# Four chained image layers on one core: the layer norms' inverse deviations are spread by DMA, and the last image's pointwise products use 64x64 array tiles

## The chip, the cores and the metric

The kernel runs on one core of a Trainium2 chip. The metric is the time of one execution in microseconds, measured on the device. Before the change it is 2722.68 us, the median of three runs from 2719.42 to 2723.97.

The core's engines are named as in the profile: PE (TensorE, matrix products; PEld is its loading of weights, which overlaps), DVE (VectorE), ACT (ScalarE), POOL (GpSimd) and SP (SyncE, here only an issuer of DMAs). Each engine runs its own list of instructions in order, and waits where an operand isn't ready. SBUF is the on-chip memory of 128 partitions; PSUM holds the results of PE.

## The reference, cut to what matters

Four images of 64x64 positions with 64 channels go through four layers. Layers 0, 2 and 3 are attention over the 4096 positions of an image (in layer 2 a position's row and column play the parts of space and channel as the reference reshapes them). Layer 1, which is changed here, is a convolution block with two layer norms:

```python
def _ln(x, g, b):
    m = jnp.mean(x, axis=-1, keepdims=True)
    v = jnp.mean(jnp.square(x - m), axis=-1, keepdims=True)
    return (x - m) * jax.lax.rsqrt(v + EPS) * g + b

y = _ln(x, ln1_g, ln1_b)
y = _pw(y, pw1_w, pw1_b)              # 64 -> 256 channels at each position
y = _dw3x3(y, dw_w, dw_b)
y1, y2 = jnp.split(y, 2, axis=-1)
y = y1 * y2
w = jnp.mean(y, axis=(1, 2), keepdims=True)
w = _pw(w, sca_w, sca_b)
y = y * w
y = _pw(y, pw2_w, pw2_b)
x = x + y * beta
z = _ln(x, ln2_g, ln2_b)
z = _pw(z, pw3_w, pw3_b)              # 64 -> 256 channels
z1, z2 = jnp.split(z, 2, axis=-1)
z = z1 * z2
z = _pw(z, pw4_w, pw4_b)
return x + z * gamma
```

All data is float32.

## The kernel before

An image is kept as X[:, b], 128 partitions by 2048 columns: partitions 0 to 63 are the 64 channels of one half of the positions, partitions 64 to 127 those of the other half. A group of 512 columns is called j (0 to 3), a half s (0 or 1), and tok(x, s, j) takes one such block of 64 partitions by 512 columns.

The kernel has two paths: fast_path, which is what runs here, and a general path that is taken only if a check of value ranges at the end fails. Everything below is fast_path.

The order of work on PE, ACT and DVE is written out by a program-level scheduler. A main list, items, holds the attention work: a layer 0 item is the scores of 128 positions (L1008, then exponentials L1012 on ACT), a layer 2 item the scores L1207 with exponentials L1215, a layer 3 item L1321 with L1326. Work that is due some items later (products L1032, L1224, L1348; evictions of accumulators, L1039 on DVE; the scaling vq, L1021 to L1024 on DVE) is put behind the item it is due at. Beside the list two lanes, conv and misc, are generators whose yield says how many units of about a microsecond to let pass before their next piece. After an item's scores and again after its due work, each lane ticks by the item's own number of units and issues the pieces whose time has come. conv runs layer1(b) for the four images one after another, starting when image b's layer 0 is through its items; it runs beside layer 0 of the next image, and for the last images beside layer 2. misc runs the preparation of the attention layers: project0, features2 (which copies ko between halves by DMA on SP, L1190), close2 and open3 (which copies keys ph from tg by DMA on SP, L1295).

PE works on parts of its array. A product with 64 rows of weights uses one row half, so that two of them (s = 0 and 1) run beside each other: "64*128" in the profile's lines. Layer 2's scores and products use quarters, "64*64", four beside each other. In layer 0 the scores are 64*128 and the products 128*64.

PSUM has three buffers of 128x1024 for scores and everything else (new_ps) and two of 128x512 for attention's accumulators (new_acc). In SBUF, tiles t and u share two buffers (new_t), and xn has one.

The norm (called twice in layer1) works so: ACT squares X (L1058); PE sums X and its squares over the channels with the matrix jsel, 1/64 in column s for the partitions of half s (L1064), which leaves means and mean squares at rows 32j+s of a PSUM tile; ACT, DVE and ACT turn these into the inverse deviation (L1069 to L1072), at rows 32j+s of t. To multiply a channel, the inverse deviation of its positions has to be on that channel's partition. PE does this with the matrix bsel, the transpose of the selection sel: for each j it multiplies 32 rows of bsel with 32 rows of t (L1078), which gives a 128x512 block, two blocks per PSUM tile. DVE then multiplies the PSUM tile with X into xn (L1083). The mean itself isn't subtracted there; it is folded into the weights pw1 and pw3 in setup (cmat, L903).

The pointwise products that follow are L1103 (pw1, written to the padded tile by ACT at L1108, then convolved by DVE at L1123 and L1125) and L1160 (pw3, joined by ACT L1165 and DVE L1167 into u; then pw4, L1171). Each uses, for one j and one half r of the outputs, two matmuls of 64 weight rows by 128 outputs, one for each s.

In the profile a float32 matmul appears as two instructions.

Of the kernel before, what the change touches and what calls it, by code (L numbers as in the profile page):

```python
# [8 lines left out]
F32 = mybir.dt.float32  # L9
# [682 lines left out]
def fast_path(ctx: ExitStack, tc: tile.TileContext, a: dict, out: bass.AP, bad):  # L692
    nc = tc.nc
    B, H, W, C = a["x"].shape
# [4 lines left out]
    const = ctx.enter_context(tc.tile_pool(name="const", bufs=1))  # L699
# [11 lines left out]
    def new_ps(name="ps"):  # L711
        return pp.tile([128, 1024], F32, tag="ps", name=name)
# [7 lines left out]
    def new_t(name="t"):  # L720
        return tp.tile([128, 1024], F32, tag="t", name=name)
# [7 lines left out]
    mm = nc.tensor.matmul  # L729
# [8 lines left out]
    def fetch_x(b, queues):  # L738
# [19 lines left out]
        out=gam0, in_=a["L0_conv_gamma"].rearrange("(o n) -> o n", o=1).to_broadcast([128, 1])  # L758
# [3 lines left out]
    ident = const.tile([128, 128], F32, name="ident")  # L762
# [40 lines left out]
    for nm in names128:  # L803
        r = flat[nm].shape[0] // 128
        nc.sync.dma_start(
            out=rows[col[nm] : col[nm] + r, :], in_=flat[nm].rearrange("(r c) -> r c", r=r)
        )
    for nm in names64 + names32:
        n = flat[nm].shape[0]
        nc.sync.dma_start(  # L810
            out=rows[col[nm] : col[nm] + 1, :].rearrange("o (d n) -> o d n", n=n),
            in_=flat[nm].rearrange("(r d n) -> r d n", r=1, d=1).to_broadcast([1, 128 // n, n]),
# [11 lines left out]
    pw1 = blocks("pw1", "L1_conv_pw1_w", 256, [(0, 0), (1, 0)], 256)  # L824
# [16 lines left out]
    bqk = const.tile([128, 1], F32, name="bqk")  # L841
    cmat = const.tile([128, 128], F32, name="cmat")
    nc.gpsimd.memset(cmat, 0.0)
    sel = new_t("sel")[:, 0:128]
    nc.gpsimd.memset(sel, 0.0)
    for s in range(2):
        nc.gpsimd.memset(cmat[64 * s : 64 * s + 64, 64 * s : 64 * s + 64], -1.0 / C)
        nc.gpsimd.memset(sel[64 * s : 64 * s + 64, s:128:32], 1.0)
    jsel = const.tile([128, 32], F32, name="jsel")
    bsel = const.tile([128, 128], F32, name="bsel")  # L850
    eps1 = const.tile([128, 1], F32, name="eps1")
    nc.gpsimd.memset(eps1, EPS1)
    eps3 = const.tile([128, 1], F32, name="eps3")
# [22 lines left out]

    def setup():
        nc.vector.tensor_add(cmat, cmat, ident)
        nc.vector.tensor_scalar_mul(jsel, sel[:, 0:32], 1.0 / C)
        ps = new_ps()  # L880
        nc.tensor.transpose(ps[:, 0:128], sel, ident)
        nc.tensor.transpose(ps[:, 512 : 512 + n_rows], rows, ident[:n_rows, :n_rows])
        nc.vector.tensor_copy(bsel, ps[:, 0:128])
        nc.vector.tensor_copy(vec, ps[:, 512 : 512 + n_rows])
        yield 5.0

        ps = new_ps()
        for i, (w_, sh, bi) in enumerate(
            ((pw1, "L1_conv_ln1_b", "L1_conv_pw1_b"), (pw3, "L1_conv_ln2_b", "L1_conv_pw3_b"))
        ):  # L890
            for r in range(2):
                mm(
                    ps[:, 2 * i + r : 2 * i + r + 1], w_[0:64, bass.ts(r, 128)], V(sh, 0, 0, 64),
                    start=True, stop=True,
                )
            nc.vector.tensor_add(
                pwb[:, i, :], ps[:, 2 * i : 2 * i + 2], vec[:, col[bi] : col[bi] + 2]
            )

        ps = new_ps()  # L900
        for i, (w_, g) in enumerate(((pw1, "L1_conv_ln1_g"), (pw3, "L1_conv_ln2_g"))):
            nc.vector.tensor_scalar_mul(w_, w_, V(g))
            mm(ps[:, 512 * i : 512 * i + 256], cmat, w_, start=True, stop=True)  # L903
            nc.vector.tensor_copy(w_, ps[:, 512 * i : 512 * i + 256])
        nc.vector.tensor_mul(resb[:, 0:1], V("L1_conv_pw2_b"), V("L1_conv_beta"))
        nc.vector.tensor_mul(resb[:, 1:2], V("L1_conv_pw4_b"), V("L1_conv_gamma"))
        yield 3.0
# [15 lines left out]
    def tok(x, s, j):  # L923
        return x[64 * s : 64 * s + 64, bass.ts(j, 512)]
# [128 lines left out]
    def norm(x, y):  # L1053


        sq = [new_t("sq"), new_t("sq")]
        for i in range(2):
            act(sq[i], x[:, bass.ts(i, 1024)], AF.Square)  # L1058
        yield 4.0
        ps = new_ps()  # L1060
        for i, src in enumerate(((x, x), (sq[0], sq[1]))):
            for j in range(4):
                c = 512 * j if i == 0 else 512 * (j % 2)
                mm(  # L1064
                    ps[32 * j : 32 * j + 32, bass.ts(i, 512)], jsel, src[j // 2][:, c : c + 512],
                    start=True, stop=True,
                )
        t = new_t()
        act(t[:, 0:512], ps[:, 0:512], AF.Square)  # L1069
        stt(t[:, 0:512], t[:, 0:512], -1.0, ps[:, 512:1024], ALU.mult, ALU.add)  # L1070
        act(t[:, 0:512], t[:, 0:512], AF.Ln, bias=eps1)
        act(t[:, 512:1024], t[:, 0:512], AF.Exp, scale=-0.5)  # L1072
        yield 7.0
        for jp in range(2):
            ps = new_ps()
            for i in range(2):
                p = 32 * (2 * jp + i)
                mm(  # L1078
                    ps[:, bass.ts(i, 512)], bsel[p : p + 32, :], t[p : p + 32, 512:1024],
                    start=True, stop=True,  # L1080
                )
            cols = bass.ts(jp, 1024)
            nc.vector.tensor_mul(y[:, cols], ps, x[:, cols])  # L1083
            yield 3.5

    def layer1(b):
        x = X[:, b]
        y = xn.tile([128, 2048], F32, tag="xn", name="xn")
        yield from norm(x, y)
        yg = new_big("yg")[:, 0:N].rearrange("p (w h) -> p w h", h=H)  # L1090
        ysum = sm.tile([128, 4], F32, tag="ysum", name="ysum")
        for r in (1, 0):
            pad = new_pad()
            nc.gpsimd.memset(pad[:, 0:PW], 0.0)
            nc.gpsimd.memset(pad[:, 65 * PW : 66 * PW + 2], 0.0)
            nc.gpsimd.memset(
                pad[:, PW : 65 * PW].rearrange("p (w h) -> p w h", h=PW)[:, :, 0:1], 0.0
            )
            inner = pad[:, PW + 1 : 65 * PW + 1].rearrange("c (p q s h) -> c q p s h", p=2, s=2, h=PW)
            for j in range(4):  # L1100
                ps = new_ps()
                for s in range(2):
                    mm(  # L1103
                        ps[:, bass.ts(s, 512)], pw1[64 * s : 64 * s + 64, bass.ts(r, 128)],
                        tok(y, s, j), start=True, stop=True,
                    )
                for s in range(2):
                    act(  # L1108
                        inner[:, bass.ts(j, 4), :, s, 0:H],
                        ps[:, bass.ts(s, 512)].rearrange("c (q p h) -> c q p h", p=2, h=H),  # L1110
                        AF.Identity, bias=pwb[:, 0, r : r + 1],
                    )
                yield 3.5
            for j in range(4):
                w0 = 16 * j
                y2 = yg[:, w0 : w0 + 16, :]
                out_ = y2 if r else new_t("y1").rearrange("p (w h) -> p w h", h=H)
                for k in range(9):
                    o = (w0 + k % 3) * PW + k // 3
                    win = pad[:, o : o + 16 * PW].rearrange("p (w h) -> p w h", h=PW)[:, :, 0:H]  # L1120
                    wt = V("L1_conv_dw_w", 2 * k + r)
                    if k == 0:
                        nc.vector.tensor_scalar(out_, win, wt, V("L1_conv_dw_b", r), ALU.mult, ALU.add)  # L1123
                    else:
                        stt(out_, win, wt, out_, ALU.mult, ALU.add)  # L1125
                    yield 1.8
                if not r:
                    stt(y2, out_, 1.0, y2, ALU.mult, ALU.mult, accum_out=ysum[:, j : j + 1])
                    yield 1.8
# [3 lines left out]
        ps = new_ps()  # L1133
# [6 lines left out]
        for j in range(4):  # L1140
            ps = new_ps()
# [13 lines left out]
        for j in range(4):  # L1155
            t, u = new_t(), new_t("u")
            for r in range(2):
                ps = new_ps()
                for s in range(2):
                    mm(  # L1160
                        ps[:, bass.ts(s, 512)], pw3[64 * s : 64 * s + 64, bass.ts(r, 128)],
                        tok(z, s, j), start=True, stop=True,
                    )
                if r == 0:
                    act(t, ps, AF.Identity, bias=pwb[:, 1, 0:1])  # L1165
                else:
                    stt(u, ps, pwb[:, 1, 1:2], t, ALU.add, ALU.mult)  # L1167
                yield 3.5
            ps = new_ps()
            for s in range(2):  # L1170
                mm(ps[64 * s : 64 * s + 64, 0:512], pw4, u[:, bass.ts(s, 512)], start=True, stop=True)  # L1171
            act(t[:, 0:512], ps[:, 0:512], AF.Identity, bias=resb[:, 1:2], scale=V("L1_conv_gamma"))
            xs = x[:, bass.ts(j, 512)]
            nc.vector.tensor_add(xs, xs, t[:, 0:512])
            yield 3.5
# [424 lines left out]
```

## Time and profile before

| what | value |
|---|---|
| median of three runs | 2722.68 us |
| the profiled execution: its own time, its span | 2720.37 us, 2718.6 us |
| granted clock of PE, mean | 0.994 |
| norm sums L1064 on PE, X and squares | 8.5 and 8.3 us busy, 64 instructions each |
| spreading L1078 on PE | 18.0 us busy, 64 instructions |
| product L1083 on DVE | 19.5 us busy, 16 instructions of 1222 ns |
| pointwise L1103, L1160 on PE | 35.8 and 35.0 us busy, 128 instructions each |
| DMA over the whole span | 24.33 MB; queue of SP 3.1% of 16 engines' span |

The span goes from the first to the last instruction of the execution. Busy times of PE count every instant at which a matmul is under way, so that matmuls side by side count once; single durations (about 600 ns for 512 columns) overlap and can't be summed. A timeline line gives start, duration, engine, line, and how many instructions were merged; in brackets stands how long the engine was idle before, and what ended it. A windows line gives, for each engine, busy time and number of instructions in a stretch, then the granted clock of PE, the share of the DMA engines, and GB/s.

### The profile page before, as it was taken

Reading aid. Unit: us, or ns where it says so; the run is one execution under the profiler, and the core shown is the slowest. Engines: PE = TensorE matmul, PEld = TensorE weight load, DVE = VectorE, ACT = ScalarE, POOL = GpSimd, SP = SyncE. Lnnn points to the kernel's source line nnn. Section 1 sums busy time; section 2 is a strip of 40 time slices with the busy share of each in tenths; the row PEclk is TensorE's granted clock in tenths of the full one; section 3 lists DMA queues with packets and bytes.
Section 4 is the critical chain, followed back from the end, with each engine's and each line's share of the span. In section 5 each row is a group of like instructions: output and inputs, shape, how many; then the busy total and the mean of one; then the engine's idle time right before and its main releaser. Section 6 shows DMA issues by size and latency. Waiting matters only on the chain.

```text
span 2718.6 us, 41825 instructions
## 1 busy us (share of the span) xinstructions
PE 2656.8 (98%) x18042; PEld 902.6 (33%) x18042; DVE 1349.0 (50%) x1507; ACT 1724.6 (63%) x2796; POOL 16.6 (1%) x66
## 2 busy tenths in 40 slices
PE   8999999999999999999999999999999999999996
PEld 3343333333333333323333332243322333322222
DVE  3232478437773478216720027920058700088888
ACT  4545655565556555555655668855678756578886
POOL 2000000000000000000000000000000000000000
PEclk9999999999999999999999999999999999999998
DMA  3000000000000000000010000010000010010001
GB/s 71 0 1 1 1 1 1 1 1 1 1 1 1 8 8 1 1 1 17 1 32 1 16 1 1 1 32 1 17 1 1 1 32 1 1 32 1 1 1 64
DMA packets 17349, 24.33 MB, mean 9 GB/s; under 512 B 2460, under 2 KB 10885, under 8 KB 17157
## 3 DMA queue, kind: packets, MB, share of 16 engines
q1 hardware_dynamic: 16085, 20.47, 3.1%
q8 instruction: 143, 2.34, 0.4%
q0 software_dynamic: 672, 0.56, 0.1%
q10 hardware_dynamic: 400, 0.56, 0.1%
q14 instruction: 49, 0.40, 0.0%
HBM read 4.80 MB, written 4.19 MB: 3 GB/s over the span
## 4 chain that ended last, share of the span: by engine, by line
PE 94%; DVE 4%; ACT 2%; issue 0%; DMA 0%; ACTq 0%; DVEq 0%
PE acc L1032 17%; PE ps L1008 17%; PE acc L1224 16%; PE ps L1207 16%; PE ps L1321 11%; PE acc L1348 9%; PE ps L1103 1%; PE ps L1160 1%; PE accz L1337 1%; PE ps L1078 1%; PE ps L1143 1%; PE ps L1171 1%; PE ps L1064 1%; PE ps L1302 1%; PE ps L985 1%; DVE tg L1344 0%
## 5 line engine op out<-in xcount | busy, mean ns | idle before, releaser
L1012 ACT ACTIVATE e<-ps 128x1024 f32<-128x1024 f32 x512 | 517.1, 1024 | 343.4 <-PE ps L1008 231.0
L1215 ACT ACTIVATE e<-ps 128x1024 f32<-128x1024 f32 x512 | 517.1, 1024 | 308.1 <-PE ps L1207 308.0
L1326 ACT ACTIVATE e<-ps 128x1024 f32<-128x1024 f32 x512 | 495.4, 1022 | 94.9 <-PE ps L1321 85.1
L1344 DVE TENSOR_TENSOR tg<-tg,e 128x2048 f32<-128x2048 f32 x214 | 490.4, 2292 | 26.1 <-ACT e L1326 7.4
L1008 PE MATMUL ps<-X,q 64*128 64x512 f32 x2048 | 482.7, 608 | 11.3 <-ACT e L1012 4.2
L1207 PE MATMUL ps<-ko 64*64 64x512 f32 x4096 | 470.4, 593 | 7.8 <-ACT ko L1189 5.5
L1224 PE MATMUL acc<-e,X 64*64 64x512 f32 x4096 | 468.0, 591 | 2.7 <-DVE X L1039 2.1
L1032 PE MATMUL acc<-e,vq 128*64 128x512 f32 x2048 | 468.4, 599 | 0.0
L1321 PE MATMUL ps<-tg,ph 32*128 32x512 f32 x2048 | 321.2, 640 | 0.5 <-ACT e L1326 0.5
L1039 DVE SCALAR_TENSOR_TENSOR yv<-acc,gam,yv 128x512 f32<-128x512 f32 x224 | 168.0, 750 | 290.4 <-PE acc L1032 278.6
L1008 PEld LDWEIGHTS ps<-X,q 64*128 64x128 f32 x2048 | 187.0, 187 | 295.3 <-issue 190.1
L1348 PE MATMUL acc<-e,tg 128*32 128x512 f32 x2048 | 272.0, 603 | 1.3 <-ACT yz L1354 1.3
L1207 PEld LDWEIGHTS ps<-ko 64*64 64x64 f32 x4096 | 156.4, 133 | 294.7 <-issue 196.4
L1224 PEld LDWEIGHTS acc<-e,X 64*64 64x64 f32 x4096 | 159.6, 133 | 280.3 <-issue 265.0
L1032 PEld LDWEIGHTS acc<-e,vq 128*64 128x64 f32 x2048 | 136.6, 137 | 311.7 <-issue 290.3
L1232 DVE TENSOR_TENSOR ph<-ph,acc 128x512 f32<-128x512 f32 x16 | 11.0, 688 | 423.7 <-ACT ph L1231 423.7
L1321 PEld LDWEIGHTS ps<-tg,ph 32*128 32x128 f32 x2048 | 103.2, 182 | 219.2 <-issue 139.9
L1125 DVE SCALAR_TENSOR_TENSOR yg<-pad,vec,yg 128x1024 f32<-128x1024 f32 x128 | 164.3, 1283 | 5.9 <-ACT pad L1108 2.4
L1125 DVE SCALAR_TENSOR_TENSOR y<-pad,vec,y 128x1024 f32<-128x1024 f32 x128 | 164.3, 1284 | 3.7
L1348 PEld LDWEIGHTS acc<-e,tg 128*32 128x32 f32 x2048 | 43.5, 108 | 190.6 <-issue 185.1
L1215 ACT ACTIVATION_READ_ACCUMULATOR e<-ps 128x1 f32 x512 | 106.0, 207 | 0.0
L1012 ACT ACTIVATION_READ_ACCUMULATOR e<-ps 128x1 f32 x512 | 106.0, 207 | 0.0
(187 smaller groups left out, 996.5 us busy)
## 6 DMA issues: line engine op xcount, KB each, us to landing
ph<-tg SPq DMA_DIRECT2D x64, 128.0 KB
ko<-ko SPq DMA_DIRECT2D x16, 256.0 KB
out_dram<-o SPq DMA_DIRECT2D x8, 512.0 KB
xr<-in_x_dram SPq DMA_DIRECT2D x14, 256.0 KB
xr<-in_x_dram ACTq DMA_DIRECT2D x2, 256.0 KB
pw<-in_L_conv_pw_w_dram POOLq DMA_DIRECT2D x4, 64.0 KB, 4.6
sca<-in_L_conv_sca_w_dram POOLq DMA_DIRECT2D x1, 64.0 KB, 6.2
pw<-in_L_conv_pw_w_dram POOLq DMA_DIRECT2D x2, 32.0 KB, 4.8
```

The lines of the kernel that those rows point to most:

```text
L1008: mm(ps[:, bass.ts(r, 512)], m.q[rows_, bass.ts(t, 128)], x[rows_, bass.ts(g, 512)], start=True, stop=True,)
L1012: act(es[g // 2][:, bass.ts(g % 2, 1024)], ps, AF.Exp, bias=SHIFT0, accum_out=zs[:, g : g + 1],)
L1032: mm(accs[g][64 * r : 64 * r + 64, :], vq, es[half][:, 1024 * g + 512 * r : 1024 * g + 512 * r + 512], start=t == 2 * p, stop=t == 2 * p + 1,)
L1039: stt((x if p == 15 else m.y)[:, cols], accs[g], gam0, (m.y if p else x)[:, cols], ALU.mult, ALU.add,)
L1125: stt(out_, win, wt, out_, ALU.mult, ALU.add)
L1207: mm(ps[64 * c : 64 * c + 64, bass.ts(r, 512)], m.ko[rows_, 128 * jb + 64 * c : 128 * jb + 64 * c + 64], m.ko[rows_, bass.ts(2 * ib + r, 5 ...
L1215: act(es[n, jb], ps, AF.Exp, bias=SHIFT2, accum_out=m.zs[:, jb, ib : ib + 1])
L1224: mm(acc[r][64 * c : 64 * c + 64, :], xw[rows_, jb, :], es[n, jb][rows_, bass.ts(c, 512)], start=jb == 0, stop=jb == 31,)
L1321: mm(tiles[k // 2][:, bass.ts(k % 2, 512)], m.ph[rows_, bass.ts(mc, 128)], m.th[rows_, bass.ts(nb, 512)], start=True, stop=True,)
L1326: act(e[:, bass.ts(kp, 1024)], tiles[kp], AF.Exp)
L1344: nc.vector.tensor_add(esum, esum, e)
L1348: mm(st["y"][32 * k : 32 * k + 32, :], m.gx[:, mc, :], e[:, bass.ts(k, 512)], start=mc == 0, stop=mc == 31,)
```

## The change

There are two edits. In norm, the two pairs of L1078 products and their PSUM tiles are gone. SP issues eight DMAs instead, one for each j and half h: each takes one row of t (512 values on partition 32j+h) and writes it to the 64 partitions of that half in y, the tile xn. After a yield of 14 units DVE multiplies y in place with X, in two pieces of 1024 columns, with yields of 1.8 instead of 3.5. bsel is no longer needed: jsel is written directly on POOL, and setup loses a transpose and two small DVE operations.

In layer1, both pointwise layers go through a new function, pointwise. For images 0 to 2 it issues the same two matmuls as before; for the last image it splits the 128 outputs in two, which gives four matmuls of 64 rows by 64 outputs.

```diff
@@ setup of constants
-    sel = new_t("sel")[:, 0:128]
-    nc.gpsimd.memset(sel, 0.0)
+    jsel = const.tile([128, 32], F32, name="jsel")
+    nc.gpsimd.memset(jsel, 0.0)
     for s in range(2):
         nc.gpsimd.memset(cmat[64 * s : 64 * s + 64, 64 * s : 64 * s + 64], -1.0 / C)
-        nc.gpsimd.memset(sel[64 * s : 64 * s + 64, s:128:32], 1.0)
-    jsel = const.tile([128, 32], F32, name="jsel")
-    bsel = const.tile([128, 128], F32, name="bsel")
+        nc.gpsimd.memset(jsel[64 * s : 64 * s + 64, s : s + 1], 1.0 / C)
@@ def setup():
         nc.vector.tensor_add(cmat, cmat, ident)
-        nc.vector.tensor_scalar_mul(jsel, sel[:, 0:32], 1.0 / C)
         ps = new_ps()
-        nc.tensor.transpose(ps[:, 0:128], sel, ident)
         nc.tensor.transpose(ps[:, 512 : 512 + n_rows], rows, ident[:n_rows, :n_rows])
-        nc.vector.tensor_copy(bsel, ps[:, 0:128])
         nc.vector.tensor_copy(vec, ps[:, 512 : 512 + n_rows])
@@ def norm(x, y):
         act(t[:, 512:1024], t[:, 0:512], AF.Exp, scale=-0.5)
         yield 7.0
+        for j in range(4):
+            for h in range(2):
+                nc.sync.dma_start(
+                    out=y[64 * h : 64 * h + 64, bass.ts(j, 512)],
+                    in_=t[32 * j + h : 32 * j + h + 1, 512:1024].unsqueeze(1).to_broadcast([1, 64, 512]),
+                )
+        yield 14.0
         for jp in range(2):
-            ps = new_ps()
-            for i in range(2):
-                p = 32 * (2 * jp + i)
-                mm(
-                    ps[:, bass.ts(i, 512)], bsel[p : p + 32, :], t[p : p + 32, 512:1024],
-                    start=True, stop=True,
-                )
             cols = bass.ts(jp, 1024)
-            nc.vector.tensor_mul(y[:, cols], ps, x[:, cols])
-            yield 3.5
+            nc.vector.tensor_mul(y[:, cols], y[:, cols], x[:, cols])
+            yield 1.8
@@ def layer1(b):
         x = X[:, b]
+        width = 64 if b == B - 1 else 128
+
+        def pointwise(ps, w, r, src, j):
+            for o in range(0, 128, width):
+                for s in range(2):
+                    mm(
+                        ps[o : o + width, bass.ts(s, 512)],
+                        w[64 * s : 64 * s + 64, 128 * r + o : 128 * r + o + width],
+                        tok(src, s, j), start=True, stop=True,
+                    )
+
...
                 ps = new_ps()
-                for s in range(2):
-                    mm(
-                        ps[:, bass.ts(s, 512)], pw1[64 * s : 64 * s + 64, bass.ts(r, 128)],
-                        tok(y, s, j), start=True, stop=True,
-                    )
+                pointwise(ps, pw1, r, y, j)
...
                 ps = new_ps()
-                for s in range(2):
-                    mm(
-                        ps[:, bass.ts(s, 512)], pw3[64 * s : 64 * s + 64, bass.ts(r, 128)],
-                        tok(z, s, j), start=True, stop=True,
-                    )
+                pointwise(ps, pw3, r, z, j)
```

## The prediction

> **What bounds the kernel now.** I read the page first: engine shares, then the chain that ended last.
>
> ```profile
> span 2718.6 us, 41825 instructions
> PE 2656.8 (98%) x18042; PEld 902.6 (33%) x18042; DVE 1349.0 (50%) x1507; ACT 1724.6 (63%) x2796; POOL 16.6 (1%) x66
> PE 94%; DVE 4%; ACT 2%; issue 0%; DMA 0%; ACTq 0%; DVEq 0%
> ```
>
> TensorE (PE) is the bound: 98% busy, 94% of the chain, only 61.8 us idle in the span. So a matmul taken away is worth its slot on PE, and any wait on which PE stands is paid in full. VectorE is half idle over the span, but PE's accumulators are emptied by it. Next, the timeline around the first norm (image 0), which has every piece that the change touches:
>
> ```profile
> 288.47 1.06 PE L1064 MATMUL ps<-X,jsel 128*32 128x512 f32 x8
> 289.35 1.04 PE L1064 MATMUL ps<-sq,jsel 128*32 128x512 f32 x8
> 290.32 2.85 PE L1008 MATMUL ps<-X,q 64*128 64x512 f32 x12
> ...
> 292.69 0.63 ACT L1072 ACTIVATE t<-t 128x512 f32<-128x512 f32 x1
> ...
> 299.01 1.13 PE L1078 MATMUL ps<-t,bsel 32*128 32x512 f32 x4
> 300.07 3.70 PE L1008 MATMUL ps<-X,q 64*128 64x512 f32 x16
> ...
> 303.70 1.13 PE L1078 MATMUL ps<-t,bsel 32*128 32x512 f32 x4
> 304.76 1.13 PE L1103 MATMUL ps<-xn,pw 64*128 64x512 f32 x4
> ```
>
> Call T0 the end of the norm's sums on PE (290.3). The inverse deviation is ready at T0+3.0 (292.69+0.63). A pair of L1078 products holds PE for 1.06 us, start to next start (299.01 to 300.07, 303.70 to 304.76). One "step" of attention work, scores or products, is 3.6 us.
>
> Then the only copies between SBUF partitions of the size that the change adds: ph<-tg, 16 of 128 KB each. SyncE's timeline and the windows (last two columns: share of the 16 DMA engines, GB/s):
>
> ```profile
> 1396.97 11.32 SPq L1295 DMA_DIRECT2D ph<-tg  x16
> ...
> 1398.00:1400.00 2.00, 2.00 (x18) 0.66 (x12) 0.00 (x0) 0.00 (x0) 0.00 (x0) 1.00 0.80 170
> 1404.00:1406.00 2.00, 2.00 (x21) 1.10 (x22) 1.24 (x2) 0.19 (x1) 0.00 (x0) 1.00 0.95 208
> ```
>
> They go out every 0.71 us (11.32/16), data flows some 1.2 us after the first issue, at 208 GB/s at best with the engines 95% busy. Last, what a PE pause costs beyond itself, where layer 2's layout is first built (last columns: granted clock, DMA share, GB/s):
>
> ```profile
> 954.15 3.78 PE L1008 MATMUL ps<-X,q 64*128 64x512 f32 x8 [3.14 <-ACT ko L1189]
> 957.87 4.76 PE L1032 MATMUL acc<-e,vq 128*64 128x512 f32 x16
> ...
> 954.00:958.00 4.00, 3.85 (x10) 1.27 (x12) 1.54 (x2) 3.35 (x8) 0.00 (x0) 0.50 0.61 131
> 958.00:962.00 4.00, 4.00 (x14) 1.19 (x16) 0.17 (x1) 1.10 (x2) 0.00 (x0) 0.73 0.00 0
> ```
>
> After 3.1 us of idleness the clock is half: 8 matmuls take 3.78 us instead of half of 3.70, the next 16 4.76 instead of 3.65. That is 1.9+1.1 = about 3 us extra per pause.
>
> [...]ph<-tg uses 32 partitions[...], and 208 is its best window. No single-partition copy is in the trace. [...]four 64x64 quads take 3.48 us between like neighbours (1128.52 to 1132.00, 0.87 each), a lone 64x128 pair among them 1.06 (1412.85 to 1413.91).[...]
>
> **The change, part by part.**
> (1) Removed: 8 norms x 2 pairs of L1078 = 16 slots x 1.06 = -17.0 us on PE (the group's busy time is 18.0). All of it is on the path.
> (2) Setup: one transpose (0.33 us) and two small VectorE operations go: -0.5 with its start; the memsets on GpSimd are off the path.
> (3) Last image: 16 pairs become 64x64 quads. In both kernels all of image 3's pointwise work falls beside layer 2, which runs in 64x64: 16 x (1.06-0.87) = -3.0. Bounds: [...]-5 if the neighbours' steps shorten also (3.60 to 3.48).
> Sum of gains: 20.5 us.
> (4) VectorE's product reads SBUF instead of PSUM: L1083 takes 1222 ns, and an all-SBUF product of that size (L1514) 1220. Nothing.
> (5) Pacing: each norm's lane gets 14+3.6 instead of 7 units after it, two norms per image: about +21 units per image, +85 by image 3. Layer 1 ended at 1445 and so ends near 1530, before layer 3's first scores at 1609, beside which VectorE and ScalarE would be over 80% busy (108 and 110 us of the first 131). Nothing in time.
> (6) Added: 8 copies per norm of 128 KB, each one row of one partition sent to 64. SyncE issues them one behind the other, the first waiting for the exponential. The ko and ph copies of layers 2 and 3 are behind them on that queue; they are consumed tens of us later, and cost nothing.
> (7) The new wait: VectorE's two products wait for copies 1-4 and 5-8. Behind the second on VectorE are the accumulator evictions (L1039) and the scaling of vq; behind these, PE.
>
> What the copies cost is the whole question. From below: at ph<-tg's rate the last issues at T0+3.0+7x0.71 and lands 1.9 later, at T0+10. The instruction order of the changed kernel puts VectorE's products some five to seven steps after T0, 18 us or later: hidden, cost zero. From above: copies 1-4 read partitions 0, 1, 32, 33[...]; 5-8 read 64, 65, 96, 97[...]. [...]landed at T0+4.2+19.0+0.3 = T0+23.5 and T0+42.5; products done at 24.7 and 43.7. I take this end[...].
>
> PE's stalls follow from its new order (steps of 3.6, a pointwise pair 1.0, 1.2 us of ScalarE delay as at 294):
> - Norm 1: first pair wanted at 22.8, free at 24.7; a step and pair later attention products need the accumulators whose eviction is behind the second product: wanted 30.3, free 43.7+1.5 (evictions)+0.6 (vq) = 45.8. Stall 1.9+15.5 = 17.4.
> - Norms 2 and 3: seven steps before the first pair (26.4), accumulators wanted at 32.0: 13.8 each.
> - Norm 4: stops at pw4's product, wanted 35.6, its input after evictions, vq and L1167: 47.0. 11.4.
> - Norm 5: third pair wanted 35.6, ready 43.7, then 1.1 for accumulators: 9.2.
> - Norms 6 to 8, beside layer 2: only five steps before the first pair, 19.1 against 24.7: 5.6; then pw4's product or the third pair: 11.1, 10.0, 11.1. Together 16.7, 15.6, 16.7.
> Sum 114.6. Eleven of these pauses exceed 3 us: 11 x 2.9 = 32 for the clock. Total cost 147.
>
> Net: -20.5+147 = +126. The profiled execution took 2720.4 (span 2718.6): 2847 us. The median before, 2722.7, is 2 us above it, less than the scatter of its three runs.
>
> **The rivals.**
> Hidden copies: the single rows are read about as fast as ph<-tg. For it: [...]the same 2 KB is read again and again. [...]Then only the gains remain: 2720.4-20.5 = 2700, the side opposite to my forecast. It decides where the second half lands before about T0+28 (products 1.2, evictions 1.5, against 32): 1.05 MB in 24 us, some 44 GB/s.
> Partly hidden: a rate between 30 and 44, for instance if the engines run unevenly and the two halves overlap. The stall of each norm shrinks towards the 2.6 us (20.5/8) that only cancels the gains: 2700 to 2800.
> Slower than a port: [...]Each half takes 19 us more, so the last product comes 38 later: +304, about 3150. Nothing in the trace excludes it; nothing shows it.
> The copies do carry the same values as bsel did (row 32j+h to half h), so the change does what it says.
>
> **How the numbers follow.** One port 0.55 (2847, own range 2800 to 2890: clock 1 to 4 us a pause, halves overlapping a little); hidden 0.22; partly hidden 0.10; slower than a port 0.13. The range 2696 to 2890 takes in the first three and leaves out the last (0.13) and the tails (some 0.05). Faster by over 0.2% (5.4 us, what a measurement of this kernel can tell from none): 0.22. Within: 0.03, from the partly hidden case. Slower: 0.55+0.13+0.07 = 0.75.
>
> **What will show it.** In the changed profile: VectorE waiting for xn's copies, some 100 us or more in 16 waits; DMA at 25 to 30 GB/s for about 38 us from each norm's exponential; PE idle before the attention products and pointwise pairs, followed by the half clock; no L1078 matmuls. A lone quad in image 3 should hold PE about 0.87. I am wrong if the copies' windows show over 45 GB/s: then PE never waits and the time falls by about 20.

## The result, and the profile after

| | before | after |
|---|---|---|
| median | 2722.66 us (4 runs) | 2815.40 us (4 runs) |
| span of the profiled execution | 2718.6 us | 2814.0 us |
| PE busy, idle in the span | 2656.8, 61.8 us | 2660.4, 153.6 us |
| mean granted clock of PE | 0.994 | 0.975 |

The changed kernel is slower: ratio 1.0343, interval 1.0325 to 1.0361, 92.7 us. The direction and the cause were as forecast, the size was 31 to 34 us less than forecast. The page of the changed kernel, with the lines that answer to those of before:

```profile
span 2814.0 us, 41965 instructions
PE 2660.4 (95%) x18041; PEld 915.8 (33%) x18041; DVE 1347.6 (48%) x1505; ACT 1725.1 (61%) x2796; POOL 16.5 (1%) x66
PE 85%; DVE 4%; SPq 4%; DMA 3%; ACT 2%; issue 2%; ACTq 0%; DVEq 0%; POOL 0%; POOLq 0%
L1078 DVE TENSOR_TENSOR xn<-xn,X 128x1024 f32<-128x1024 f32 x16 | 19.6, 1225 | 212.9 <-DMA xn<-t 212.9
```

PE's share of the chain has fallen from 94% to 85%; SP's queue, which was not listed before, and the DMA, which was at 0%, now hold 7% of it. In front of its 16 products VectorE stands idle for 212.9 us in all and waits for the copies. (Lines have moved: L1078 is now this product, L1071 the copies, L1088 both pointwise layers, L1034 the evictions, L1165 the product u, L1003 and L1027 layer 0's scores and products.)

The first norm's copies, in SP's timeline and in the windows (last columns: granted clock, DMA share, GB/s):

```profile
293.40 26.93 SPq L1071 DMA_DIRECT2D xn<-t  x8
```

```profile
300.00:304.00 4.00, 4.00 (x20) 1.45 (x18) 0.42 (x3) 3.75 (x7) 0.00 (x0) 1.00 0.95 28
...
312.00:316.00 4.00, 1.73 (x10) 0.46 (x7) 1.47 (x2) 0.00 (x0) 0.00 (x0) 0.96 0.89 43
316.00:320.00 4.00, 4.00 (x12) 1.87 (x14) 1.55 (x5) 1.92 (x3) 0.00 (x0) 0.61 0.94 28
```

The 16 DMA engines are 95% busy and move 28 GB/s. Only where the first half of the copies ends and the second, from other rows, begins does a window show more, 43 GB/s. The eight copies take SP 26.93 us to issue, a median of 4.36 us each over all 64, where ph<-tg took 0.71: SP's issuing was slow where the copies were slow. VectorE and PE in the same norm:

```profile
314.53 1.23 DVE L1078 TENSOR_TENSOR xn<-xn,X 128x1024 f32<-128x1024 f32 x1 [6.82 <-DMA xn<-t]
315.67 1.41 DVE L1034 SCALAR_TENSOR_TENSOR yv<-acc,gam,yv 128x512 f32<-128x512 f32 x2
...
332.22 1.23 DVE L1078 TENSOR_TENSOR xn<-xn,X 128x1024 f32<-128x1024 f32 x1 [14.60 <-DMA xn<-t]
```

```profile
315.86 2.08 PE L1088 MATMUL ps<-xn,pw 64*128 64x512 f32 x4 [2.27 <-issue]
317.69 4.31 PE L1003 MATMUL ps<-X,q 64*128 64x512 f32 x16
...
322.79 3.65 PE L1027 MATMUL acc<-e,vq 128*64 128x512 f32 x16
333.55 2.08 PE L1088 MATMUL ps<-xn,pw 64*128 64x512 f32 x4 [7.10 <-issue]
335.39 5.69 PE L1003 MATMUL ps<-X,q 64*128 64x512 f32 x16
```

T0, the end of the sums on PE, is 290.4 here. The two halves are there at T0+24.1 and T0+41.8. PE stands 2.3 and 7.1 us before the first and the third pointwise pair; after each pause the scores take 4.31 and 5.69 us in place of 3.70, at a granted clock of 0.61 (316 to 320) and 0.50 (332 to 336): the half clock. In the next norm PE stands before attention's products instead, which need VectorE's evictions queued behind its second product:

```profile
584.77 5.61 PE L1027 MATMUL acc<-e,vq 128*64 128x512 f32 x16 [12.82 <-DVE yv L1034]
```

### The profile page after: what moved, and what is told of

It is laid out like the page before. It is cut to its first block, busy times and chain, and to the rows that moved or that the text cites. A ratio compares the mean times of both kernels' runs of the same rounds, so it can differ in the third digit from the quotient of the medians.

```text
span 2814.0 us, 41965 instructions
## 1 busy us (share of the span) xinstructions
PE 2660.4 (95%) x18041; PEld 915.8 (33%) x18041; DVE 1347.6 (48%) x1505; ACT 1725.1 (61%) x2796; POOL 16.5 (1%) x66
## 2 busy tenths in 40 slices
DMA packets 22471, 32.74 MB, mean 12 GB/s; under 512 B 3484, under 2 KB 11909, under 8 KB 22277
## 4 chain that ended last, share of the span: by engine, by line
PE 85%; DVE 4%; SPq 4%; DMA 3%; ACT 2%; issue 2%; ACTq 0%; DVEq 0%; POOL 0%; POOLq 0%
PE acc L1027 15%; PE acc L1222 15%; PE ps L1003 14%; PE ps L1205 14%; PE ps L1319 10%; PE acc L1346 8%; SPq L1071 4%; DMA xn<-t 3%; PE ps L1088 2%; PE accz L1335 1%; ACT e L1213 1%; DVE y L1127 1%; PE ps L1169 1%; PE ps L1145 1%; PE ps L1059 1%
## 5 line engine op out<-in xcount | busy, mean ns | idle before, releaser
L1213 ACT ACTIVATE e<-ps 128x1024 f32<-128x1024 f32 x512 | 516.7, 1024 | 309.6 <-PE ps L1205 309.5
L1003 PE MATMUL ps<-X,q 64*128 64x512 f32 x2048 | 483.7, 609 | 22.7 <-DVE u L1165 12.1
L1027 PE MATMUL acc<-e,vq 128*64 128x512 f32 x2048 | 473.0, 604 | 25.3 <-DVE yv L1034 25.3
L1034 DVE SCALAR_TENSOR_TENSOR yv<-acc,gam,yv 128x512 f32<-128x512 f32 x224 | 167.5, 750 | 290.0 <-PE acc L1027 278.6
L1003 PEld LDWEIGHTS ps<-X,q 64*128 64x128 f32 x2048 | 189.2, 188 | 307.1 <-issue 198.7
L1222 PEld LDWEIGHTS acc<-e,X 64*64 64x64 f32 x4096 | 166.9, 134 | 274.6 <-issue 256.0
L1027 PEld LDWEIGHTS acc<-e,vq 128*64 128x64 f32 x2048 | 137.7, 138 | 340.6 <-issue 290.2
L1078 DVE TENSOR_TENSOR xn<-xn,X 128x1024 f32<-128x1024 f32 x16 | 19.6, 1225 | 212.9 <-DMA xn<-t 212.9
L1088 PE MATMUL ps<-xn,pw 64*128 64x512 f32 (+1 forms) x320 | 77.3, 690 | 45.2 <-issue 45.0
L1213 ACT ACTIVATION_READ_ACCUMULATOR e<-ps 128x1 f32 x512 | 106.1, 207 | 0.0
```

Source lines behind the costliest of these rows:

```text
L1003: mm(ps[:, bass.ts(r, 512)], m.q[rows_, bass.ts(t, 128)], x[rows_, bass.ts(g, 512)], start=True, stop=True,)
L1027: mm(accs[g][64 * r : 64 * r + 64, :], vq, es[half][:, 1024 * g + 512 * r : 1024 * g + 512 * r + 512], start=t == 2 * p, stop=t == 2 * p + 1,)
L1034: stt((x if p == 15 else m.y)[:, cols], accs[g], gam0, (m.y if p else x)[:, cols], ALU.mult, ALU.add,)
L1213: act(es[n, jb], ps, AF.Exp, bias=SHIFT2, accum_out=m.zs[:, jb, ib : ib + 1])
L1222: mm(acc[r][64 * c : 64 * c + 64, :], xw[rows_, jb, :], es[n, jb][rows_, bass.ts(c, 512)], start=jb == 0, stop=jb == 31,)
```

## The experiments

Each experiment was compared with the kernel before on the same chip: e1 to e4 on one chip, where it took 2719.2 us, p1 to p4 on another, where it took 2719.3, against 2722.7 above. Differences to before are taken within these comparisons. Ratios and intervals are as recorded; a ratio is not exactly that of the two medians.

| kernel | median us | ratio to before | interval |
|---|---|---|---|
| e1, copies from 64 partitions | 2687.42 | 0.9885 | 0.9869 to 0.9902 |
| e2, one-row copies from other rows | 2688.11 | 0.9888 | 0.9872 to 0.9905 |
| e3, copies from 32 rows | 2687.21 | 0.9884 | 0.9867 to 0.9900 |
| e4, yield 28 | 2708.87 | 0.9965 | 0.9953 to 0.9978 |
| p1, pacing only | 2710.28 | 0.9968 | 0.9956 to 0.9981 |
| p2, 64x64 tiles only | 2714.78 | 0.9988 | 0.9981 to 0.9994 |
| p3, e3 without the tiles | 2691.34 | 0.9902 | 0.9886 to 0.9917 |
| p4, e3 with yield 9 | 2692.67 | 0.9905 | 0.9889 to 0.9920 |

**e1: the same bytes, read from 64 partitions.** The sums are written to 16 columns for each half, so that all rows hold usable values.

```diff
-        nc.gpsimd.memset(jsel[64 * s : 64 * s + 64, s : s + 1], 1.0 / C)
+        nc.gpsimd.memset(jsel[64 * s : 64 * s + 64, 16 * s : 16 * s + 16], 1.0 / C)
...
-                    in_=t[32 * j + h : 32 * j + h + 1, 512:1024].unsqueeze(1).to_broadcast([1, 64, 512]),
+                    in_=t[64 * h : 64 * h + 64, 512:1024],
```

> The eight copies per norm move the same bytes to the same places, but each reads 64 partitions instead of one row (the inverse deviations that arrive belong to other positions; the rest is computed as before). Theory A (the copies are slow[...], and PE pays the wait): they land about 10 us after the norm's sums, nothing waits, 2700 us, VectorE's wait for xn falls from 212.9 us to under 10. Rival D (the cost comes from having the copies at all, from their issue on SyncE, or from layer 1 being spread over more of the program): stays near 2815.

Measured: 2687.4 us. VectorE waits for xn 22.2 us in all, more than the 10 expected, but PE's idle time is 54.9 us (2685.9-2631.0), less than the 61.8 of the kernel before. SP issues the first norm's eight copies in 4.99 us instead of 26.93: 1.05 MB at 210 GB/s, as issued. The number of copies, their bytes, their destinations and the pacing are unchanged, and the loss is gone: the profiled span falls from 2814.0 to 2685.9 us, and by the two comparisons with the kernel before e1 is 92.7+31.7 = 124.5 us faster than the changed kernel. So the loss comes from where the copies read, by way of their late landing, and not from having the copies. Against before e1 gains 31.7 us where the prediction's gains sum to 20.5, which p1 to p3 take up.

**e2: one row for each copy still, but from other rows.** The rows are 0, 16, 36, 52, 72, 88, 108 and 124, in place of 0, 1, 32, 33, 64, 65, 96 and 97. With the same wide jsel as in e1:

```diff
+                p = 32 * j + 16 * h + 4 * j
                 nc.sync.dma_start(
                     out=y[64 * h : 64 * h + 64, bass.ts(j, 512)],
-                    in_=t[32 * j + h : 32 * j + h + 1, 512:1024].unsqueeze(1).to_broadcast([1, 64, 512]),
+                    in_=t[p : p + 1, 512:1024].unsqueeze(1).to_broadcast([1, 64, 512]),
                 )
```

> Each copy still reads one row[...] (partitions 32j+16h+4j; the sums are written to more columns for this, at no extra instruction). Theory A1[...]: the eight land together within 5 to 10 us of flow, no waits, about 2700. Theory A2 (a DMA engine works through the copies in order[...]): 27 GB/s as before, 4.4 us per issue, 2815 unchanged.

Measured: 2688.1 us. A2's 27 GB/s and its 2815 us did not come. A1's time did (2688 against about 2700), its absence of waits did not. From the windows of the first norm (last columns: clock, DMA share, GB/s):

```profile
294.00:296.00 2.00, 2.00 (x10) 0.66 (x12) 0.00 (x0) 2.00 (x5) 0.00 (x0) 1.00 0.99 34
296.00:298.00 2.00, 2.00 (x14) 0.57 (x8) 0.23 (x1) 0.83 (x2) 0.00 (x0) 1.00 0.89 28
298.00:300.00 2.00, 2.00 (x12) 0.78 (x10) 1.76 (x5) 0.31 (x1) 0.00 (x0) 1.00 0.65 89
...
302.00:304.00 2.00, 2.00 (x12) 0.71 (x12) 0.00 (x0) 1.82 (x4) 0.00 (x0) 1.00 0.84 29
304.00:306.00 2.00, 2.00 (x12) 0.62 (x10) 0.90 (x2) 0.00 (x0) 0.00 (x0) 1.00 0.86 96
...
310.00:312.00 2.00, 2.00 (x13) 0.58 (x9) 0.00 (x0) 1.04 (x3) 0.00 (x0) 1.00 0.48 53
```

The first 4 us run at 28 to 34 GB/s, about the changed kernel's rate; then windows show up to 96 GB/s, but not all do: one falls back to 29. It looks as if several copies were under way at once, though one queue issues them in order; the windows show the rate alone. 1.05 MB in some 17 us is 62 GB/s, above the 44 at which the prediction's waits vanish. VectorE still idles 67.1 us before xn where no waits were expected, and PE doesn't feel it: it is idle 55.0 us (2684.7-2629.7). The changed kernel's first four copies read rows 0, 1, 32 and 33, its last four 64, 65, 96 and 97, and within each half the windows show 26 to 28 GB/s; with e2's rows six of the nine windows from 294 to 312 show 53 to 96. The form of the copies is the same: e2's spread one row over 64 partitions as the slow ones do, and by their profiles the changed kernel, e1 and e2 all move 32.74 MB in 22471 packets. So in these kernels the difference lies in which rows are read, and not in that one row is spread over many partitions. What it is about the rows was not shown.

**e3: copies from 32 rows.** Wide jsel, and 16 copies of 64 KB per norm, each from 32 rows to every fourth partition.

```diff
         for j in range(4):
-            for h in range(2):
+            for r in range(4):
                 nc.sync.dma_start(
-                    out=y[64 * h : 64 * h + 64, bass.ts(j, 512)],
-                    in_=t[32 * j + h : 32 * j + h + 1, 512:1024].unsqueeze(1).to_broadcast([1, 64, 512]),
+                    out=y[r:128:4, bass.ts(j, 512)], in_=t[32 * j : 32 * j + 32, 512:1024]
                 )
```

> Each sum is written to 16 rows, and a norm has 16 copies of 64 KB, each from 32 rows[...] to every fourth partition. The result is the reference's. Under A, A1 and A2 alike the rate is that of ph<-tg, 150 GB/s or more, issue 16 x 0.6 = 10 us, landing 14 to 16 us after the sums: VectorE waits at most a few us in all, 2700 (between 2696 and 2708), faster than before. Under D: 2815 or more, since there are twice as many copies.

Measured: 2687.2 us, ratio 0.9884 (0.9867 to 0.9900), faster than both kernels and below the expected band. Unlike e1 it puts the right value on every partition. VectorE waits for xn 38.3 us in all, where a few were expected; PE, idle 54.6 us, doesn't feel it. The first norm's copies, in SP's timeline and in the windows:

```profile
294.28 10.08 SPq L1071 DMA_DIRECT2D xn<-t  x16
```

```profile
296.00:298.00 2.00, 2.00 (x12) 0.63 (x10) 0.00 (x0) 2.00 (x5) 0.00 (x0) 1.00 0.39 98
...
302.00:304.00 2.00, 2.00 (x10) 0.58 (x8) 0.00 (x0) 2.00 (x5) 0.00 (x0) 1.00 0.42 107
```

They go out every 0.63 us (10.08/16), the DMA engines are only 40% busy: here the issue sets the rate, 64 KB per 0.63 us is 104 GB/s, and the windows from 296 to 304 show 98 to 107. Twice as many copies as in e1 cost nothing that the times show (2687.2 against 2687.4 us).

**e4: the slow copies, but VectorE comes later for them.**

```diff
-        yield 14.0
+        yield 28.0
```

> The copies as in the changed kernel, but the yield after them is 28 instead of 14, so that VectorE's products come some four steps of attention work later, about when the second half lands (41.8 us after the sums). Theory A (all the loss is waiting): the copies still flow at 27 GB/s, VectorE waits under 40 us in all, PE hardly at all: 2700 to 2715. Layer 1 ends some 110 us later than in the changed kernel and runs into the first 30 us of layer 3, which may cost up to 10 of it. If the copies' flow itself disturbs PE, or the longer lane costs, it stays over 2750.

Measured: 2708.9 us, within the expected band. The copies go out as slowly as ever (27.03 us of issue in the first norm), and yet in layer 0 PE has no pause over 2 us any more: the flow of the copies by itself doesn't stop PE. VectorE waits 70.5 us, more than the 40 expected; in the later norms its longest wait for xn is 22.6 us, and PE stands 5.92 us before the product with u at 1253, 5.17 before a pointwise quad at 1342 and 3.31 before another product with u at 1549. A pause of 3.14 us before a ko copy at 1180 is there too, of the kind that p1 takes up. Against e3 the medians are 22 us apart; of the 19.6 us between the profiled spans PE is idle for 14.8 (69.4 against 54.6) and busy for 4.8, so these four pauses and the slow work after some of them can account for the difference.

**p1 to p3: where the gains come from.** e1 to e3 are 31 to 32 us faster than before, the prediction's sum of gains is 20.5. p1 gives the kernel before the changed kernel's yields and keeps every L1078:

```diff
         act(t[:, 512:1024], t[:, 0:512], AF.Exp, scale=-0.5)
         yield 7.0
+        yield 14.0
         for jp in range(2):
...
             nc.vector.tensor_mul(y[:, cols], ps, x[:, cols])
-            yield 3.5
+            yield 1.8
```

> The kernel before with all its L1078 products, but with the changed kernel's yields (14 more after the exponential, 1.8 instead of 3.5 after each piece). Theory P (some 12 us of the 32 that the changes without the wait bring are due to layer 1 coming later beside the attention work, because pauses of PE like the 3.1 us at 954 before ScalarE's ko copy, and the half clock after it, go): 2707 to 2711, 8 to 12 us faster. Rival Q (they come from the products themselves, that is a removed pair is worth nearly 2 us instead of 1.06): unchanged within 2 us of the kernel before.

Measured: 9.0 us faster (ratio 0.9968, 0.9956 to 0.9981, so 5 to 12 us). Theory P holds, Q does not. The two pauses before ScalarE's ko copies in the kernel before, and the same two places in p1:

```profile
954.15 3.78 PE L1008 MATMUL ps<-X,q 64*128 64x512 f32 x8 [3.14 <-ACT ko L1189]
...
1238.45 3.69 PE L1207 MATMUL ps<-ko 64*64 64x512 f32 x16 [4.51 <-ACT ko L1189]
```

```profile
938.28 2.27 PE L1008 MATMUL ps<-X,q 64*128 64x512 f32 x8 [0.89 <-ACT ko L1190]
...
1202.19 2.23 PE L1208 MATMUL ps<-ko 64*64 64x512 f32 x16 [0.93 <-ACT ko L1190]
```

5.8 us of pausing have gone there, and with it the half clock (granted 0.50 in 954 to 958 and in 1238 to 1242 before, 1.00 in p1 in 930 to 940 and in 1196 to 1206): 8 matmuls after the first pause take 2.27 instead of 3.78 us, 16 after the second 2.23 instead of 3.69. In all p1's PE is 6.2 us less idle (2706.1-2650.5 = 55.6 against 61.8) and 6.3 us less busy. (These are two single executions, whose spans differ by 12.5 us; the medians differ by 9.0.)

p2 is the kernel before with pointwise as in the changed kernel, nothing else:

```diff
+        width = 64 if b == B - 1 else 128
...
-                for s in range(2):
-                    mm(
-                        ps[:, bass.ts(s, 512)], pw1[64 * s : 64 * s + 64, bass.ts(r, 128)],
-                        tok(y, s, j), start=True, stop=True,
-                    )
+                pointwise(ps, pw1, r, y, j)
```

and the same for pw3. p3 is e3 with

```diff
-        width = 64 if b == B - 1 else 128
+        width = 128
```

> The kernel before with the last image's pointwise products in 64x64 tiles, nothing else. Prediction's sum: 16 x 0.19 = 3.0 us faster, with bounds 0 and 5. Seen as 2714 to 2719 against about 2719. A rival in which the twice as many matmuls cost their issue: slower by up to 2.

> The kernel with copies from 32 rows, without the 64x64 tiles. If the tiles are worth 3 us there too: 2690 against 2687. If they are worth nothing there, 2687.

Measured: p2 is 3.3 us faster by the ratio (0.9988, 0.9981 to 0.9994, so 1.6 to 5.2 us) and 4.5 by the medians; p3 is 4.1 us slower than e3, in the same sense though its interval overlaps e3's and it ran on the other chip. So the tiles are worth 3 to 5 us in both places. The timeline of e3 shows two lone quads of image 3, that of p3 the pairs in their place:

```profile
1233.95 3.61 PE L1221 MATMUL acc<-e,X 64*64 64x512 f32 x32
1237.38 3.61 PE L1204 MATMUL ps<-ko 64*64 64x512 f32 x32
1240.82 1.04 PE L1087 MATMUL ps<-xn,pw 64*64 64x512 f32 x8
1241.67 3.61 PE L1221 MATMUL acc<-e,X 64*64 64x512 f32 x32
1245.11 1.04 PE L1087 MATMUL ps<-xn,pw 64*64 64x512 f32 x8
1245.96 3.86 PE L1204 MATMUL ps<-ko 64*64 64x512 f32 x32
1249.74 1.09 PE L1087 MATMUL ps<-xn,pw 64*64 64x512 f32 x8
```

```profile
1239.16 1.13 PE L1087 MATMUL ps<-xn,pw 64*128 64x512 f32 x4
1240.22 3.67 PE L1221 MATMUL acc<-e,X 64*64 64x512 f32 x32
1243.81 1.13 PE L1087 MATMUL ps<-xn,pw 64*128 64x512 f32 x4
1244.87 3.73 PE L1204 MATMUL ps<-ko 64*64 64x512 f32 x32
1248.53 1.13 PE L1087 MATMUL ps<-xn,pw 64*128 64x512 f32 x4
```

From start to next start a quad holds PE 0.85 us, a pair 1.06. The attention products between take 3.44 us beside quads and 3.59 beside pairs, but the scores 3.78 against 3.66. Over two pointwise products and two attention steps it is 8.92 us (1240.82 to 1249.74) against 9.37 (1239.16 to 1248.53): 0.22 us for each quad, and if all 16 did the same, 3.6 us.

**p4: how much of the 14 units e3 needs.**

```diff
-        yield 14.0
+        yield 9.0
```

> The kernel with copies from 32 rows, with a yield of 9 instead of 14 after them. The copies land about 16 us after the sums and the products would come one to two steps earlier, some 12 to 18 after them: VectorE's waits grow (38.3 us in all with 14), PE still loses at most 1 to 2 us per norm. Under P a shorter lane may also bring back a pause at a ko copy (5 us). Expected 2687 to 2705; 2687 if there is slack left.

Measured: 2692.7 us, 5.5 us more than e3, within the band; the two intervals still overlap. VectorE waits less than with 14 (24.3 us against 38.3), not more as expected, so longer waits for the copies are not the cause. PE pauses elsewhere: 4.11 us in open3 at 1354, where e3 has 1.93, and 1.33 at 1065, where e3 has none. These make 3.5 of the 4.0 us by which p4's PE is idle longer than e3's (58.6 against 54.6). p4 wasn't split further.

## Why the prediction was right, and where its sizes were off

**The bound and the waiting: right.** For the copies' cost the prediction took the end that it calls one port: each half of the copies (524 KB) takes 19.0 us, one half behind the other. The 19.0 us were the author's assumption; nothing in the trace before showed a copy from a single row. While the copies of one half flow, the windows show 26 to 28 GB/s; the landings are at T0+24.1 and T0+41.8 against 23.5 and 42.5. e1 and e2 change only where the copies read (and fill more rows to read from) and take the whole loss away.

**Stalls of PE: right in kind, 18 us too many.** Pauses over 2 us by the brackets in PE's timeline, each norm from its sums on:

| norm | 1 | 2 | 3 | 4 | 5 | 6 | 7 | 8 | sum |
|---|---|---|---|---|---|---|---|---|---|
| predicted us | 17.4 | 13.8 | 13.8 | 11.4 | 9.2 | 16.7 | 15.6 | 16.7 | 114.6 |
| measured us | 9.4 | 12.8 | 12.5 | 12.1 | 7.1 | 14.7 | 12.6 | 15.8 | 97.0 |

They are nearly all of the 99.0 us by which PE is idle longer than in e3. Norm 1 is a misreading: the prediction put the evictions of the step before behind VectorE's second product, but in VectorE's order they stand between the two; PE went on one step further and stopped at the third pointwise pair. In norms 6 to 8, which pause twice, the first pause is longer than the 5.6 us of the working (8.0, 6.7 and 8.0): in norm 6 PE comes to it 17.3 us after T0 instead of 19.1, since its five steps take about 3.43 us each there and not 3.6. The second is shorter, 6.7, 5.9 and 7.8 us against 11.1, 10.0 and 11.1. Two things shorten it. The halves land 17.7 us apart and not 19.0, and the half clock after the first pause stretches the work before the second: in norm 6 two pairs and two steps take 12.3 us between the pauses, at full clock 9.4 (p3 above). The sum counted the slow work and the full wait.

**The clock: right in size.** 32 us were charged for eleven pauses over 3 us, and eleven such pauses came, the shortest of 5.89 us. Against e3, which differs by the copies and the wide jsel alone, PE is busy 29.4 us longer (2660.4-2631.0) and idle 99.0 us longer (153.6-54.6): 128.4 us, the whole difference of the spans. After each of the eleven the next work ran slow (7.10 us of pause, then 5.69 for a step of 3.70). After shorter pauses it went either way: 2.27 us were enough here for a step of 4.31, while after 3.31 us in e4, at 1549, the next step took 3.67. What decides in that range stays open. The prediction's total cost was 147.

**The gains: 12 us too few.** The removed pairs and the setup were summed as 17.5 us, the tiles as 3.0 (measured 3 to 5). The tiles' 3.0 rests on a small misreading: the step of 3.48 us at 1128.52 stands behind the norm's sums; between like neighbours a step takes 3.43 (e3, 1233.95 to 1237.38). The pacing, step (5), was set down as "Nothing in time". It is the step that failed: it looked at where layer 1 ends and not at what its pieces stand beside, and p1 measured it at 9.0 us alone. The products can be read from p1 and p3, which ran on one chip, have the same pacing and no quads, and differ in how the inverse deviations are spread: 2710.3-2691.3 = 18.9 us for products and setup together, close to the 17.5. With 9.0 for the pacing and 3.3 for the tiles that makes 31.2 of the 32.0 us that e3 gains.

**The balance.** 147-20.5 = +126 was forecast. Measured were a cost of 128 (spans) and a gain of 32 (e3 against before), +96; the result itself is +92.7. The result lies in the range that the prediction gave its case of one port, 2800 to 2890, 15 us above its lower end. The two errors, stalls too long and gains too small, point the same way, so no luck made them cancel.

**The rivals.** Hidden copies: excluded by the changed kernel's own windows, and what they would bring shown by e1. Partly hidden: 26 to 28 GB/s is under the 30 at which it begins; the one window of 43 does not change the landings. Slower still (3150 us): excluded by the same windows. The change did what it says.

## What to carry to other kernels

Before a DMA takes over a broadcast from PE, measure the rate with the rows that it will read, and don't count the bytes alone: here copies of one row each gave 26 to 28 GB/s from rows 0, 1, 32 and 33, with the 16 DMA engines about 90% busy, 62 on average from e2's eight rows, and copies of 32 rows about 100, where the issue was the limit. Here the replication that made the source wide was free: the matmuls that write the sums take 8.5 and 8.3 us in e3 as in the changed kernel, with 32 filled columns as with one per half. When PE at 98% waits for a transfer, add the half clock after each long pause (here all eleven of 5.89 us and more); but where a second wait for the same stream of copies follows, take the slowed work off that wait. And a pacing yield that seems to cost nothing moves every later piece against the other work; measure it alone before its gain is put down to something else.

## What had not been expected of the hardware

One-row copies of one SP queue ran at 62 GB/s on average in e2 and at up to 96 in a window, where the changed kernel's had 26 to 28, with the same bytes and form and only other rows. Nor was e2's rate even: one window in the middle fell back to 29. SP's own issuing was slow behind slow copies: a median of 4.36 us for each issue, against 0.60 in e1. And the half clock after a pause was no matter of the pause's length alone: a step was slow after 2.27 us in the changed kernel and not after 3.31 in e4.
